# Layer 1 attention: the sums of the softmax over keys, taken by VectorE and transfers in place of a TensorE matmul

## The chip, the cores and the metric

The kernel runs on one core of a Trainium2 chip. The core has five engines with queues of their own: TensorE (PE in the profile; its weight loads are PEld), VectorE (DVE), ScalarE (ACT), GpSimd (POOL) and SyncE (SP, which here only issues transfers). Each queue is worked off in its order; an instruction that waits holds up those behind it. The metric is the time of one execution in microseconds of the device, the median of several runs.

## The reference, cut to what matters

Two gated layers work on x of shape (4, 1024, 512). Each adds to x the product of an attention branch and a feed-forward branch. The change touches the attention of layer 1 alone:

```python
q, k, v = (proj(wq), proj(wk), proj(wv))          # 16 heads of 32
q, k = apply_rope(q, k, sin, cos)
att = jnp.einsum('bhqd,bhkd->bhqk', q, k) * (1.0 / math.sqrt(HD))
att = jax.nn.softmax(att, axis=-1)
y = jnp.einsum('bhqk,bhkd->bhqd', att, v)
return y.transpose(0, 2, 1, 3).reshape(b, t, c) @ wo.T
```

The softmax divides by the sum over keys of exp(score - maximum). The kernel multiplies the exponentials with v first and divides afterwards, so it needs that sum for every head and query, as an inverse that stands in the layout of y.

## The kernel before, in words

**Units and steps.** The attention of layer 1 is cut into 32 units, (batch b, group g of 4 heads, half qh of the 1024 queries), in the order of the list `units` (L1085). Two units of the same heads are called a pair here: an even one (qh 0) and an odd one (qh 1). A unit has 8 steps, `TB`; one loop over s (L1110) runs through the 256 steps and 13 more, and the order of TensorE's instructions is the order in which this loop writes them. The order on the other engines and on the transfer queues is set by a planner, which lets a ready instruction of later in the program go first, except where `keep_in_program_order` pins one.

**A step on TensorE.** In step s come: the scores sq of unit s // 8 (`top`, L998), four heads in two tiles, from which VectorE takes the maxima over keys (L1011); y for the step e - 1 = s - 13 (`weigh`, L1052); one piece of a projection chain; the transposed scores sk of step e = s - 12 (`expo`, L1030), from which a second matmul with the maxima mT (L1043) subtracts and of which ScalarE takes the exponentials pT (L1048); three more pieces of the chain. `LAG` is 12. Where no chain is at hand, a step has none of these pieces.

**Chains.** `must` holds the projections of the next heads (wk and wq in two halves each, then v in two: six chains a pair), `spare` the output projections `wo_out` (L964) of a finished batch and half. A chain fills two steps. `left` (L1131) allows two output chains a pair; those that `soon` names for a step become available there. A wk or wq chain ends with a copy on ScalarE, eight small transfers on SP that swap rope's halves (L916), a product on VectorE (L919) and two operations on GpSimd (L920, L921).

**Buffers.** PSUM holds eight banks: `ring`, three tiles of two banks, taken in turn by sq and sk; `acc1`, one bank, for all chains; and one for y. The exponentials pT have three buffers in SBUF, the partial sums `part` two.

**The sums over keys.** For each unit GpSimd adds the eight pT tiles (128 keys x 4 heads x 512 queries) in seven additions (L1077, L1079), so that `part` holds, for each of 128 key rows, one partial sum. In step 6 of the unit after next (`zu`, L1192) TensorE finishes: `total` (L944) multiplies `part` by a matrix of ones, head by head, which leaves the sum over the 128 rows in z, already repeated on the 32 partitions that y has for this head. z stands in `acc1` (for the last of these units in `ring`). `divide` (L952) copies it to SBUF on ScalarE, inverts it on VectorE in four instructions of 128 columns, and GpSimd multiplies y's copy `yr` by it:

```python
zs = p2.tile([P, 512], F32, tag="zs", name=f"zs_{b}_{g}_{qh}", bufs=1)
nc.scalar.copy(zs, z)
...
    nc.vector.reciprocal(zs[:, cols], zs[:, cols])
nc.gpsimd.tensor_tensor(yT, yr, zs, ALU.mult)
```

This is so for units 0 to 29. The last two (`u >= nu - 2`) are summed on TensorE within their own steps. The maxima mT go a way that the change uses too: VectorE turns square blocks of 32 (L1016), four transfers write them to DRAM (`turned_d`, L1023), four read them back in the layout that is wanted (L1026).

Of the kernel before, what the change touches and what calls it, by code (L numbers as in the profile page):

```python
# [12 lines left out]
F32 = mybir.dt.float32  # L13
# [3 lines left out]
ALU = mybir.AluOpType  # L17
AX = mybir.AxisListType

P = 128  # L20
B, N, D = 4, 1024, 512
NT = B * N
H, HD = 16, 32
# [12 lines left out]
def kernel(ctx, tc, ins, out):  # L36
    nc = tc.nc
# [3 lines left out]
    dram = ctx.enter_context(tc.tile_pool(name="dram", bufs=1, space=bass.MemoryType.DRAM))  # L41
# [47 lines left out]
    def shared_tile(tag, name):  # L89
        return w0.tile([P, KD, D], F32, tag=tag, name=name)  # L90
# [155 lines left out]
    with ExitStack() as es:  # L246
# [4 lines left out]
        p2 = es.enter_context(tc.tile_pool(name="a0", bufs=2, reuse_waits="tile"))  # L251
# [318 lines left out]
    with ExitStack() as es:  # L570
# [3 lines left out]
        p2 = es.enter_context(tc.tile_pool(name="f0", bufs=2, reuse_waits="tile"))  # L574
# [126 lines left out]
        for g in range(NH0 * NBLK + 2 + 2 * TPB):  # L701
            blk, c = divmod(g, NH0)
            if g == NH0 * NBLK:

                for n in ("wk", "wq", "wv"):
# [3 lines left out]
                            out=W[n], in_=ins[n + "T"].rearrange("(k p) n -> p k n", p=P)  # L709
# [8 lines left out]
            for i in range(TPB):  # L718
                q = g - 2 - 2 * i
# [95 lines left out]
    with ExitStack() as es:  # L815
        wp = es.enter_context(tc.tile_pool(name="a1c", bufs=1, reuse_waits="tile"))
        p2 = es.enter_context(tc.tile_pool(name="a1", bufs=2, reuse_waits="tile"))

        def ring(name):
            return pp.tile([P, 2, 512], F32, tag="ring", name=name, bufs=3)  # L820

        def acc1(name):
            return pp.tile([P, 512], F32, tag="acc1", name=name)

        TB = N // P
# [4 lines left out]
        def load1(b):  # L830
            xnTs[b] = xpair(f"xnT1_{b}")
            for h in range(2):
                load = nc.sync.dma_start(
                    out=xnTs[b][h],
                    in_=xnT_d[b].rearrange("k p n -> p k n")[:, :, h * BLK : (h + 1) * BLK],
                )
                if b:
                    tc.keep_in_program_order(load)
# [7 lines left out]
        turned_d = [  # L846
            dram.tile([8, 512], F32, tag=f"turned{i}", name=f"turned_d{i}") for i in range(2)
        ]

        partner = []  # L850
        for i in range(2):
# [92 lines left out]
        def total(z, part, kb, n):  # L944

            for h in range(4):
                nc.tensor.matmul(  # L947
                    z[h * HD : (h + 1) * HD, :], lhsT=ones[:, :HD], rhs=part[:, h, :],
                    start=(kb == 0), stop=(kb == n - 1),
                )  # L950

        def divide(u, yr, z):  # L952

            b, g, qh = u
            zs = p2.tile([P, 512], F32, tag="zs", name=f"zs_{b}_{g}_{qh}", bufs=1)
            nc.scalar.copy(zs, z)
            yT = p2.tile([P, 512], F32, tag=f"yT{qh}", name=f"yT_{b}_{g}_{qh}", bufs=5 + qh)
            for c in range(TPB):
                cols = slice(c * P, (c + 1) * P)
                nc.vector.reciprocal(zs[:, cols], zs[:, cols])  # L960
            nc.gpsimd.tensor_tensor(yT, yr, zs, ALU.mult)
            yTs[b][g, qh] = yT
# [29 lines left out]
        def advance(parts):  # L992
            nonlocal chain
            for _ in range(parts):
                if chain is not None:
                    next(chain)
# [88 lines left out]
        units = [(b, g, qh) for b in range(B) for g in range(4) for qh in range(2)]  # L1085
        nu, LAG = len(units), TB + 4
        yTs = {b: {} for b in range(B)}
# [18 lines left out]
            tc.tile_pool(name="psuma", bufs=1, space=PSUM, reuse_waits="tile")  # L1106
        )
        must, spare = deque(), deque()
        mx, mTs, pTs, ys, parts, lates, soon = {}, {}, {}, {}, {}, {}, {}
        for s in range(TB * nu + LAG + 1):  # L1110

            e = s - LAG
            if s % (2 * TB) == 0 and s < TB * nu:

                assert not must
                n = s // (2 * TB) + 1
                if n < 4 * B:  # L1120
                    b, g = divmod(n, 4)

                    two = (nc.sync, nc.gpsimd) if s == 0 else (nc.sync, nc.sync)
                    must.extend(
                        heads_in(
                            b, g, acc1, {(w, h): two for w in ("wk", "wq") for h in range(2)}
                        )
                    )
                    if g == 3 and b + 1 < B:
                        load1(b + 1)  # L1130
                left = 2  # L1131
            if s in soon and s < TB * nu:
                spare.extend(wo_out(*soon.pop(s), acc1))
            if s % 2 == 0:

                chain = None
                if spare and left and s < TB * nu:
                    chain = spare.popleft()
                    left -= 1
                elif must:  # L1140
                    chain = must.popleft()
            if s == 2 * TB:
                W["wo"] = shared_tile("wo", "wo")
                tc.keep_in_program_order(
                    nc.sync.dma_start(
                        out=W["wo"], in_=ins["woT"].rearrange("(k p) n -> p k n", p=P)
                    )
                )
            if s % 4 == 0 and s // 4 < TPB:
                lates[s + 2] = s // 4, late(s // 4)  # L1150
            if s < TB * nu:
                u, j = divmod(s, TB)
                if j == 0:
                    mx[u] = p2.tile([P, TPB, 4, 2], F32, tag="mx", name=f"mx_{u}")
                for pair in range(2):
                    top(u, j, pair, mx[u])
                if j == TB - 1:
                    m2 = twice[u % 2][:, :, :8].rearrange("p q (h c) -> p q h c", c=2)

                    w = p2.tile([P, TPB, 4, 2], F32, tag="m1", name=f"m1_{u}")  # L1160
                    nc.vector.tensor_reduce(
                        w[:, :, :, 0], mx.pop(u), AX.X, ALU.max, negate=True
                    )
                    for out, sign in ((w[:, :, :, 1], -1.0), (m2[:, :, :, 0], 1.0)):
                        nc.scalar.activation(
                            out.bitcast(F32R), w[:, :, :, 0], AF.Copy, scale=sign
                        )
                    nc.vector.tensor_reduce(m2[:, :, :, 1], w, AX.X, ALU.add)
            late_exp = s >= TB * nu
            if late_exp:  # L1170
                exps(e)
            if 1 <= e <= TB * nu:
                u, kb = divmod(e - 1, TB)
                if kb == 0:
                    ys[u] = pp.tile([P, 512], F32, tag="y", name=f"y_{u}")
                weigh(u, kb, pTs[e - 1], ys[u])
                if u >= nu - 2:

                    if kb == 0:
                        z_last = acc1(f"z_{u}")  # L1180
                    if u < nu - 1 or kb < TB // 2:
                        total(z_last, pTs[e - 1], kb, TB)
                pTs.pop(e - 2, None)
                if kb == TB - 1:
                    yr = p2.tile([P, 512], F32, tag="yr", name=f"yr_{u}", bufs=1)
                    nc.scalar.copy(yr, ys[u])
                    ys[u] = yr
                    if u == nu - 2:
                        divide(units[u], ys.pop(u), z_last)
                        soon[s] = units[u][0], units[u][2], yTs[B - 1]  # L1190
            held = 0
            zu = (s - 6) // TB - 2  # L1192
            if s % TB == 0 and 0 < s <= TB * nu:
                turn_max(s // TB - 1)
            if s % TB == 6 and 0 <= zu < nu - 2:
                z = ring(f"z_{zu}")[:, 0, :] if zu == nu - 3 else acc1(f"z_{zu}")
                total(z, parts.pop(zu), 0, 1)
                divide(units[zu], ys.pop(zu), z)
                b, g, qh = units[zu]
                if g == 3:  # L1200
                    soon[s + 4] = b, qh, yTs[b]
            elif s in lates:
                late_turn(*lates.pop(s))
            else:
                held = 1
                advance(1)
            if not late_exp:
                exps(e)
            advance(4 - held)
            if TB * nu - 12 <= s < TB * nu:  # L1210

                nxt = weight(raw1, w0, True)
                if loaded:
                    loaded()
                loaded = nxt
                if s == TB * nu - 1:
                    loaded()

        soon = [*soon.values()]
# [307 lines left out]
```

## Time and profile before

| | us |
|---|---|
| median of 3 runs | 3089.14 (3086.78 to 3090.99) |
| the profiled execution | 3092.08 |
| its span, first to last instruction | 3090.2 |

| stretch of the span, us | PE | PEld | DVE | ACT | POOL |
|---|---|---|---|---|---|
| 600 to 1100 (end of layer 0) | 491.68 | 392.27 | 366.88 | 271.45 | 213.73 |
| 1300 to 1600 (attention, layer 1) | 296.69 | 115.07 | 166.93 | 127.87 | 265.14 |
| 1600 to 2000 | 400.00 | 159.46 | 220.57 | 171.10 | 342.99 |
| 2000 to 2500 | 497.84 | 198.38 | 277.11 | 218.16 | 436.26 |
| 2500 to 3090 (its end, feed-forward) | 574.63 | 434.80 | 329.63 | 201.75 | 60.30 |

The granted TensorE clock is 0.996 of full speed over the span. Columns are microseconds in which the engine was busy in that stretch. Matmuls are pipelined, so their spans overlap and a busy PE says nothing of how much it gets done. In lines of the timeline the columns are start, duration (both us), engine, line, operation, written and read tiles, shapes, count; in brackets stands the idle time ahead of the instruction and what ended it. In lines of groups, behind the bar: busy us, mean ns of one, idle us ahead of them and what ended most of it.

### The profile page before, as it was taken

How to read it: one execution, taken by the hardware profiler on the slowest of the kernel's cores; microseconds unless marked ns; L12 is line 12 of the kernel's file. 1: busy time of each engine (PE TensorE's matmuls, PEld its weight loads, DVE VectorE, ACT ScalarE, POOL GpSimd, SP SyncE). 2: the span in 40 equal slices, each digit the busy share in tenths (PEclk: the TensorE clock that was granted, in tenths of full speed). 3: DMA queues.
4: the chain of work that ended last, by engine and by line, in shares of the span. 5: the costliest groups of instructions: out<-in, count | busy, mean ns of one | idle time of the engine just before them, and what ended most of it. 6: DMA issues, size and time to landing. Idle time of an engine off the chain costs nothing.

```text
span 3090.2 us, 61139 instructions
## 1 busy us (share of the span) xinstructions
PE 3038.3 (98%) x25985; PEld 1730.5 (56%) x25985; DVE 1788.3 (58%) x2569; ACT 1173.7 (38%) x1708; POOL 1557.9 (50%) x742
## 2 busy tenths in 40 slices
PE   9999999999999998999999999999999999999998
PEld 5555555578788873333334444333434436888886
DVE  4444555467777776555555555555555544566655
ACT  3111111145556542444444444444444454333332
POOL 1221212234443444888888988888988940001001
PEclk9999999999999999999999999999999999999999
DMA  4222232323223231100001000100000014222111
GB/s 137 86 86 86 86 86 72 127 96 100 95 92 110 96 129 52 36 9 9 9 18 42 16 10 15 43 16 14 10 18 15 13 46 152 82 69 75 58 52 56
DMA packets 113787, 186.81 MB, mean 60 GB/s; under 512 B 19809, under 2 KB 33633, under 8 KB 113377
## 3 DMA queue, kind: packets, MB, share of 16 engines
q1 hardware_dynamic: 106096, 161.30, 17.3%
q0 software_dynamic: 7280, 21.39, 1.9%
q8 instruction: 205, 3.36, 0.5%
q14 instruction: 78, 0.63, 0.1%
q10 hardware_dynamic: 128, 0.13, 0.0%
HBM read 115.11 MB, written 59.26 MB: 56 GB/s over the span
## 4 chain that ended last, share of the span: by engine, by line
PE 57%; DVE 1%; ACT 1%; POOL 1%; issue 0%; SPq 0%; DMA 0%; ACTq 0%; POOLq 0%; DVEq 0%
PE sk L1037 9%; PE sq L1007 8%; PE y L1056 8%; PE gate L1260 5%; PE up L1260 5%; PE dn L1282 5%; PE wo L862 4%; PE v1ps L862 3%; PE wk L862 3%; PE wq L862 3%; PE sk L1043 2%; PE z L947 1%; ACT pT L1048 1%; DVE zs L960 1%; POOL part L1079 0%; DVE mx L1011 0%
## 5 line engine op out<-in xcount | busy, mean ns | idle before, releaser
L1011 DVE TENSOR_REDUCE mx<-sq 128x2 f32<-128x1024 f32 x512 | 604.2, 1218 | 434.8 <-PE sq L1007 434.0
L1079 POOL TENSOR_TENSOR part<-part,pT 128x2048 f32<-128x2048 f32 x180 | 817.8, 4543 | 17.3 <-ACT pT L1048 8.9
L1048 ACT ACTIVATE pT<-sk 128x1024 f32<-128x1024 f32 x512 | 495.6, 1020 | 557.3 <-PE sk L1043 520.1
L1007 PE MATMUL sq<-wkT,wqT 32*128 32x512 f32 x2048 | 321.0, 639 | 10.0 <-ACT pT L1048 7.0
L1037 PE MATMUL sk<-wqT,wkT 32*128 32x512 f32 x2048 | 322.8, 641 | 0.8 <-DVE mx L1011 0.5
L1056 PE MATMUL y<-pT,v 128*32 128x512 f32 x2048 | 275.5, 608 | 0.1
L1304 POOL TENSOR_TENSOR th<-th,x 128x512 f32<-128x512 f32 x31 | 40.1, 1293 | 458.0 <-DVE th L1303 379.0
L646 PE MATMUL pj<-wpj,hp 128*128 128x512 f32 x1024 | 262.0, 396 | 4.0 <-DVE hp L606 4.0
L593 PE MATMUL fc<-xp,wfc 128*128 128x512 f32 x1024 | 259.0, 395 | 3.6 <-ACT h L598 2.8
L614 POOL TENSOR_TENSOR sums<-sums,h 128x512 f32<-128x512 f32 x112 | 163.1, 1456 | 195.0 <-ACT h L598 189.7
L1043 PE MATMUL sk<-mT,onesr 2*128 2x512 f32 x1024 | 235.7, 788 | 0.0
L382 PE MATMUL qk<-xnT,wqkv 128*128 128x512 f32 x512 | 228.7, 600 | 0.7 <-ACT xnT L156 0.7
L646 PEld LDWEIGHTS pj<-wpj,hp 128*128 128x128 f32 x1024 | 191.2, 188 | 51.9 <-DVE hp L606 10.5
L593 PEld LDWEIGHTS fc<-xp,wfc 128*128 128x128 f32 x1024 | 189.4, 188 | 47.2 <-ACT h L598 6.0
L606 DVE TENSOR_TENSOR hp<-h,hp 128x512 fp32r<-128x512 f32 x128 | 128.2, 1001 | 85.2 <-ACT hp L603 85.2
L1260 PE MATMUL gate<-xp,wf 128*128 128x512 f32 x704 | 174.2, 390 | 0.0
L1260 PE MATMUL up<-xp,wf 128*128 128x512 f32 x704 | 173.9, 389 | 0.0
L1037 PEld LDWEIGHTS sk<-wqT,wkT 32*128 32x128 f32 x2048 | 96.2, 184 | 138.3 <-issue 117.2
L1282 PE MATMUL dn<-wf,hp 128*128 128x512 f32 x704 | 173.6, 390 | 0.0
L1077 POOL TENSOR_TENSOR part<-pT,pT 128x2048 f32<-128x2048 f32 x30 | 136.4, 4548 | 72.1 <-ACT pT L1048 72.0
L1007 PEld LDWEIGHTS sq<-wkT,wqT 32*128 32x128 f32 x2048 | 89.9, 184 | 122.7 <-issue 85.5
L382 PEld LDWEIGHTS qk<-xnT,wqkv 128*128 128x128 f32 x512 | 95.0, 191 | 111.8 <-issue 104.5
(230 smaller groups left out, 4359.3 us busy)
## 6 DMA issues: line engine op xcount, KB each, us to landing
s<-s SPq DMA_DIRECT2D x96, 256.0 KB
xp<-xp_d SPq DMA_DIRECT2D x16, 1024.0 KB
x<-x SPq DMA_DIRECT2D x36, 256.0 KB
x<-in_x SPq DMA_DIRECT2D x32, 256.0 KB
raw_fc<-in_w_fcT SPq DMA_DIRECT2D x32, 256.0 KB
xp_d<-hi POOLq DMA_DIRECT2D x32, 256.0 KB, 2.7
xp_d<-xnT POOLq DMA_DIRECT2D x32, 256.0 KB, 2.9
x0r<-in_x SPq DMA_DIRECT2D x32, 256.0 KB
```

The lines of the kernel that those rows point to most:

```text
L382: nc.tensor.matmul(a, lhsT=wqkv[k][:, c0 : c0 + P], rhs=xnTs[blk][:, k, :], start=(k == 0), stop=(k == KD - 1),)
L593: nc.tensor.matmul(a, lhsT=wfc[k][:, c * P : (c + 1) * P], rhs=xp[n][:, k, :].bitcast(F32R), start=(k == 0 and n == 0), stop=(k == KD - 1 ...
L646: nc.tensor.matmul(ds[i], lhsT=hparts[blk, c][n][:, i * P : (i + 1) * P], rhs=wpj[c], start=(c == 0 and n == 0), stop=(c == NH0 - 1 and n ...
L862: nc.tensor.matmul(out[r0 : r0 + HD, :], lhsT=lhsT[:, r0 : r0 + HD], rhs=rhs, start=start, stop=stop,)
L1007: nc.tensor.matmul(sq[:, hh, :], lhsT=qT[r, q0 : q0 + P], rhs=kT[r, n * 512 : (n + 1) * 512], start=True, stop=True,)
L1011: nc.vector.tensor_reduce(mx[:, qt, 2 * pair : 2 * pair + 2, n], sq, AX.X, ALU.max)
L1037: nc.tensor.matmul(sks[h // 2][:, h % 2, :], lhsT=kT[r, kb * P : (kb + 1) * P], rhs=qT[r, qh * 512 : (qh + 1) * 512], start=True, stop=False,)
L1048: nc.scalar.activation(pT[:, 2 * pair : 2 * pair + 2, :], sks[pair], AF.Exp, scale=QKS)
L1056: nc.tensor.matmul(y[r, :], lhsT=v[:, kb, r], rhs=pT[:, h, :], start=(kb == 0), stop=(kb == TB - 1),)
L1079: add.tensor_tensor(parts[u], parts[u], pT, ALU.add)
L1260: nc.tensor.matmul(a, lhsT=ws[n, c][:, k, :], rhs=xp[m][:, k, :], start=(k == 0 and m == 0), stop=(k == KD - 1 and m == 1),)
L1282: nc.tensor.matmul(ds[i], lhsT=hparts[blk, c][n][:, i * P : (i + 1) * P], rhs=w, start=(c == 0 and n == 0), stop=(c == NH1 - 1 and n == 1),)
```

## The change

For units 0 to 29 the matmul z, its copy and the four inverses are dropped. In their place, spread over steps from step 6 of the unit after next on (the same step in which z stood):

- `sums_of`, eight times a unit (two in step 6, then 1, 1, 2, 1, 1 in the steps after it): VectorE turns 256 of the 2048 columns of `part` in square blocks of 32, so that queries lie on partitions and the 32 key rows of one group of partitions lie in a row, and sums those rows to 8 columns of `groups`.
- `gather`, six steps after the first: VectorE turns `groups` back, a transfer writes it to DRAM (32 KB), and a second brings the four groups of key rows beside each other on 32 partitions.
- `invert`, two steps later: VectorE sums the four groups and inverts 64 columns; a transfer writes them to DRAM, and four transfers spread each head's 512 inverses on its 32 partitions (`partition_broadcast`).
- `times`, two steps later again: GpSimd's multiplication, as before.

So a unit's yT is there ten steps later than it was written before, and `soon` names the output chains for eight steps later. In the last pair `left` is 8. `yr` gets two buffers for one; `divide` stays for the last two units, with its zs in the buffers of mT.

```diff
+        groups_d = [dram.tile([P, 64], F32, tag=f"groups{i}", name=f"groups_d{i}") for i in range(2)]
+        inverse_d = [
+            dram.tile([2, HD, HD], F32, tag=f"inverse{i}", name=f"inverse_d{i}") for i in range(2)
+        ]
...
+        def sums_of(u, part, c):
+
+            if c == 0:
+                groups[u] = p2.tile([P, 64], F32, tag="groups", name=f"groups_{u}", bufs=1)
+            t = p2.tile([P, 256], F32, tag="keys", name=f"keys_{u}_{c}", bufs=1)
+            nc.vector.transpose(t, part.rearrange("p h q -> p (h q)")[:, c * 256 : (c + 1) * 256])
+            nc.vector.tensor_reduce(
+                groups[u][:, 8 * c : 8 * c + 8], t.rearrange("p (c a) -> p c a", a=HD), AX.X, ALU.add
+            )
+
+        def gather(u):
+            back = p2.tile([P, 64], F32, tag="back", name=f"back_{u}", bufs=1)
+            nc.vector.transpose(back, groups.pop(u))
+            at = groups_d[u % 2]
+            nc.sync.dma_start(out=at, in_=back)
+            sides[u] = p2.tile([P, 256], F32, tag="keys", name=f"sides_{u}", bufs=1)
+            nc.sync.dma_start(
+                out=sides[u][:HD, :].rearrange("c (i x) -> c i x", i=4),
+                in_=at.rearrange("(i c) x -> c i x", i=4),
+            )
+
+        def invert(u):
+            b, g, qh = units[u]
+            inv = p2.tile([P, 64], F32, tag="inv", name=f"inv_{u}", bufs=1)
+            nc.vector.tensor_reduce(
+                inv[:HD, :], sides.pop(u)[:HD, :].rearrange("c (i x) -> c x i", i=4), AX.X, ALU.add
+            )
+            nc.vector.reciprocal(inv[:HD, :], inv[:HD, :])
+            at = inverse_d[u % 2]
+            nc.sync.dma_start(
+                out=at.rearrange("a c b -> c a b"),
+                in_=inv[:HD, :].rearrange("c (a b) -> c a b", a=2),
+            )
+            zss[u] = p2.tile([P, 512], F32, tag="zs", name=f"zs_{b}_{g}_{qh}", bufs=1)
+            for h in range(4):
+                row = at[h // 2, 16 * (h % 2) : 16 * (h % 2) + 16, :]
+                nc.sync.dma_start(
+                    out=zss[u][h * HD : (h + 1) * HD, :],
+                    in_=row.rearrange("c b -> (c b)").partition_broadcast(HD),
+                )
+
+        def times(u, yr):
...
+            nc.gpsimd.tensor_tensor(yT, yr, zss.pop(u), ALU.mult)
+            yTs[b][g, qh] = yT
...
-            zs = p2.tile([P, 512], F32, tag="zs", name=f"zs_{b}_{g}_{qh}", bufs=1)
+            zs = p2.tile([P, 512], F32, tag="mT", name=f"zs_{b}_{g}_{qh}")
...
-                left = 2
+
+                left = 2 if n < 4 * B else TB
...
+            zu, at = divmod(s - 6, TB)
+            zu -= 2
+            for u, i in ((zu - 1, at + TB), (zu, at)):
+                if 0 <= u < nu - 2:
+                    if i < 6:
+                        for c in ((0, 1), (2,), (3,), (4, 5), (6,), (7,))[i]:
+                            sums_of(u, parts[u], c)
...
+                    elif i == 6:
+                        gather(u)
+                    elif i == 8:
+                        invert(u)
+                    elif i == 10:
+                        times(u, ys.pop(u))
+                        b, g, qh = units[u]
+                        if g == 3:
+                            soon[s + 2] = b, qh, yTs[b]
...
-                    yr = p2.tile([P, 512], F32, tag="yr", name=f"yr_{u}", bufs=1)
+                    yr = p2.tile([P, 512], F32, tag="yr", name=f"yr_{u}")
...
-            zu = (s - 6) // TB - 2
...
-            if s % TB == 6 and 0 <= zu < nu - 2:
-                z = ring(f"z_{zu}")[:, 0, :] if zu == nu - 3 else acc1(f"z_{zu}")
-                total(z, parts.pop(zu), 0, 1)
-                divide(units[zu], ys.pop(zu), z)
-                b, g, qh = units[zu]
-                if g == 3:
-                    soon[s + 4] = b, qh, yTs[b]
-            elif s in lates:
+            if s in lates:
```

More of the change, by code (lines that the diff above doesn't have):

```diff
@@ L952, in divide @@
+        def times(u, yr):
+            b, g, qh = units[u]
+            yT = p2.tile([P, 512], F32, tag=f"yT{qh}", name=f"yT_{b}_{g}_{qh}", bufs=5 + qh)
+            nc.gpsimd.tensor_tensor(yT, yr, zss.pop(u), ALU.mult)
+            yTs[b][g, qh] = yT
         def divide(u, yr, z):
             b, g, qh = u
-            zs = p2.tile([P, 512], F32, tag="zs", name=f"zs_{b}_{g}_{qh}", bufs=1)
+            zs = p2.tile([P, 512], F32, tag="mT", name=f"zs_{b}_{g}_{qh}")
             nc.scalar.copy(zs, z)
@@ L1108 @@
         must, spare = deque(), deque()
+        groups, sides, zss = {}, {}, {}
         mx, mTs, pTs, ys, parts, lates, soon = {}, {}, {}, {}, {}, {}, {}
@@ L1168 @@
                     nc.vector.tensor_reduce(m2[:, :, :, 1], w, AX.X, ALU.add)
+            zu, at = divmod(s - 6, TB)
[5 more added lines that the diff above has]
+                            sums_of(u, parts[u], c)
+                        if i == 5:
+                            parts.pop(u)
+                    elif i == 6:
[4 more added lines that the diff above has]
+                        times(u, ys.pop(u))
+                        b, g, qh = units[u]
+                        if g == 3:
+                            soon[s + 2] = b, qh, yTs[b]
             late_exp = s >= TB * nu
```

## The prediction

> **What bounds the kernel now.** I read the page first, then the timeline of layer 1's attention (1162 to 2570 us of the span) engine by engine, then its groups of instructions with shapes kept apart, then the waits.
>
> ```profile
> PE 3038.3 (98%) x25985; PEld 1730.5 (56%) x25985; DVE 1788.3 (58%) x2569; ACT 1173.7 (38%) x1708; POOL 1557.9 (50%) x742
> PE sk L1037 9%; PE sq L1007 8%; PE y L1056 8%; PE gate L1260 5%; PE up L1260 5%; PE dn L1282 5%; PE wo L862 4%; PE v1ps L862 3%; PE wk L862 3%; PE wq L862 3%; PE sk L1043 2%; PE z L947 1%; ACT pT L1048 1%; DVE zs L960 1%; POOL part L1079 0%; DVE mx L1011 0%
> ```
>
> PE sets the end nearly everywhere, and the two things that the change takes away, the matmul z (L947) and the inverses (L960), each have about 1% of the chain. What a piece of PE work is worth is read from the steps: every step begins with the matmuls sq, so the distance between two such starts is its length.
>
> ```profile
> 1821.50 1.14 PE L1007 MATMUL sq<-wkT,wqT 32*128 32x512 f32 x8
> 1826.76 1.14 PE L1007 MATMUL sq<-wkT,wqT 32*128 32x512 f32 x8
> 1828.71 1.04 PE L947 MATMUL z<-part,ones 128*32 128x512 f32 x8
> 1832.87 1.14 PE L1007 MATMUL sq<-wkT,wqT 32*128 32x512 f32 x8
> ...
> 1782.21 1.14 PE L1007 MATMUL sq<-wkT,wqT 32*128 32x512 f32 x8
> 1788.42 1.14 PE L1007 MATMUL sq<-wkT,wqT 32*128 32x512 f32 x8
> ...
> 1804.69 1.14 PE L1007 MATMUL sq<-wkT,wqT 32*128 32x512 f32 x8
> 1810.47 1.14 PE L1007 MATMUL sq<-wkT,wqT 32*128 32x512 f32 x8
> ...
> 2494.70 1.02 PE L1007 MATMUL sq<-wkT,wqT 32*128 32x512 f32 x4
> ```
>
> Odd unit 15: 5.26 us without z, 6.11 with it, and again 5.25 after it (next start 1838.12). Even unit 14: its z step takes 6.21, but there a wk or wq chain has just ended, and such a step takes 5.78 without z too. The last line begins a step with no projection chain, and the next start is at 2499.29: 4.59 us, held not by PE's work but by the three-buffer ring (sq waits for the exponentials). With z two such steps take 5.45 and 5.28 (starts at 1303.49, 1308.94, 1314.22).
>
> **What is removed: 24.1 us.** I read the starts of all 256 steps. (a) Even units 2 to 28: 14 x (6.21 - 5.78) = 6.0. (b) Odd units 11 to 29 outside the idle steps: 10 x (6.12 - 5.24) = 8.8, and unit 19's z step took 7.07, so 1.0 more. (c) Units 3, 5, 7, where z falls into chainless steps: 3 x (5.45 + 5.28 - 2 x 4.59) = 4.6. (d) Output chains start later (steps 82, 146, 210 for 74, 138, 202), so two of them leave pair 4 (units 8, 9) and come in pair 15. Unit 9 was 43.4; with four chainless steps like unit 3's, less z, it is 38.9, but the first step of unit 10 becomes 6.7 for 5.2 as after unit 3: 3.0 gained. (e) Unit 30 gets two more chains: eight steps of 5.24 and a transition step of 3.59 for 44.5 before: 1.0 lost. (f) Unit 31's z step, 6.31 against 4.59: 1.7. The ACT copy of z (0.585) and 128 - 8 inverses go too; their worth is inside these differences.
>
> **What VectorE gains and loses.** The rows:
>
> ```profile
> L1011 DVE TENSOR_REDUCE mx<-sq 128x2 f32<-128x1024 f32 x512 | 604.2, 1218 | 434.8 <-PE sq L1007 434.0
> ...
> L960 DVE RECIPROCAL zs<-zs 128x128 f32<-128x128 f32 x128 | 108.3, 908 | 35.7 <-ACT zs L956 35.7
> ...
> L1016 DVE STREAM_TRANSPOSE mt<-m 128x128 f32<-128x128 f32 x32 | 10.0, 312 | 3.0
> ...
> 1786.26 3.38 DVE L960 RECIPROCAL zs<-zs 128x128 f32<-128x128 f32 x4
> 1789.60 2.35 DVE L1011 TENSOR_REDUCE mx<-sq 128x2 f32<-128x1024 f32 x2
> ```
>
> The reduce of the maxima takes 1218 ns for 1024 elements and L1161, a reduce of 32, takes 186: a slope of (1218 - 186)/(1024 - 32) = 1.04 ns an element, so 256 elements take 0.42. No transpose of 256 columns is in the trace; it lies between 0.31 (L1016, 128) and 0.69 (L919, 512 columns), and with the reduces' slope at 0.45. Eight pairs: 8 x 0.87 = 6.9 a unit. The back transpose of 64 columns is 0.25, the second reduce 0.42, the inverse of 64 columns (between 0.18 for 4, L121, and 0.91 for 128) 0.5. Dependent instructions stand 0.09 apart (L1168 to L1016 at 1792.46): some 1.6. Together 9.7 for 3.4 of inverses, 6.3 more per unit. VectorE idles 2.88 a step ahead of mx, 23 a unit, so the sum is covered. The cover that matters is the single step: in step 6 of a unit two pairs (1.9) and the inverting (1.1) come to 3.0. The block of 3.38 in the fence above is a bound: mx followed it 0.1 late, and the next step was 5.24. That z step was 0.4 to 0.9 longer than the new ones, so I take 0.1 a unit for 26 units (0 to 0.6), and for the four units in chainless steps, where an mx 3.39 late did show (L960 at 1308.57 is in the chain of waits), 0.8 each: 5.8 us in all.
>
> [...]
>
> **The transfers.** Seven DMAs per unit are put on SP's queue, and two of its waits are new: the read of groups_d waits for its write, the four spreads wait for inverse_d. The nearest row is the transfer of the maxima, and for what a queue loses behind a transfer, a rope product on POOL:
>
> ```profile
> 1793.07 2.77 SPq L1023 DMA_DIRECT2D turned_d<-mt  x4
> 1797.08 0.85 SPq L1026 DMA_DIRECT2D mT<-turned_d  x3
> 1804.83 1.27 POOL L920 TENSOR_TENSOR rr<-rr,cs 128x512 f32<-128x512 f32 x1 [1.61 <-DMA rr<-raw_wk]
> ```
>
> A write's issue takes 0.66, and 1.24 after the last one the read goes out: 1.9. A rope transfer lands 1.45 after its last issue of 0.62 (1788.80 to 1790.25): 2.1. So back transpose, write and read are 0.25 + 1.9 + 2.1 = 4.3 us, the second trip with its four reads 1.9 + 4 x (0.25 to 0.66) + 1.5 = 4.4 to 6.0. The code puts two steps, 10.5 us, between gather and invert, and between invert and times. Eight rope issues in front (5.4) still fit: 9.7. SP is busy 32 us of a pair's 87 (32 rope issues, two turnings); 4.2 to 7.1 a unit more is room enough, and moves one rope half by about 0.7. In the last units SP also waits on weight buffers (up to 6.2 us each, L777): 2 us.
>
> [...]
>
> But order in a queue is not program order: the turning transpose L1016, written behind a step's mx, ran ahead of them. If invert is put before an mx and its transfer lands later, mx and then PE stand. The lower bound is 0 (the trip above fits). The upper one is POOL's L920, which waited for transfers 32 of 54 times, 74.6 us in the waits view, 2.3 each. I take 0, nearest to the trip that fits, and keep 30 x 2.3 = 70 for the range. The sums wait for part as z did (12 waits of 0.5), from a queue where mx stands behind them: inside the same bounds.
>
> **POOL** keeps its multiply (1.27). A pair costs it 14 x 4.54 + 10 x 1.27 = 76 us, with a pair now 85.9: it stays covered while its waits stay under 9; today they are about 10 of 87, half of them for want of work.
>
> **Sum.** 24.1 - 5.8 - 2 = 16. Profiled execution 3092.1 (span 3090.2) - 16 = 3076. It stood 2.9 above the median 3089.1, which makes 3073.
>
> **The rivals.** *More is gained* (0.06): the idle steps lose the stalls behind the inverses too, 4 x (6.7 - 5.2) = 6, and nothing is given back: 3089 - 24 - 6 = 3059 or below, to 3054. For it: 6.7 comes four times right after 3.39 us of inverses. Against: the same step waits for the exponentials.
> *Nothing* (0.09): times waits in POOL's queue as L920 does. In odd units the adds already run up to 8.8 us behind their exponentials, and three pT buffers allow about 11; 2.3 more can stall each of 14 pairs by 1.2: 16, 3089. Against: two steps of distance, and the lag drains in every pair.
> *Slower* (0.37): VectorE's queue stands at the second reduce, or at the first transpose of part, with the next mx behind it and then the ring. Sign turns at 16/30 = 0.53 us of PE stall per unit, 0.2% slower at 0.74. Half of L920's wait and a little, 1.3 us, gives 39: 3112; all of it 3143. For it: VectorE serves PE within 0.1 us and now waits for transfers and for POOL. Against: 2.88 us idle in every step, half the price is swallowed there.
>
> **How the numbers follow.** Forecast (0.48): 3073, own range 3057 to 3083, which leaves its costs between 0 and 18. From the slower case the range takes in all but its last third, from the larger gain most: 3056 to 3128. A measurement of this kernel tells 0.2% (6 us) from no change: 3083 to 3095 is the same. Faster 0.54, same 0.09, slower 0.37.
>
> **What would show it.** z leaves the chain; sq starts in step 6 come 5.24 (odd) and 5.78 (even) apart; L960 is 8 instructions; VectorE's new pieces are near 0.43. I am wrong if mx gets idle time released by a DMA or by POOL's part, and sq or sk by mx, of over 0.5 us a unit; or if transposes of 256 take over 0.6.

## The result, and the profile after

| | before | after |
|---|---|---|
| median, us (6 runs each) | 3091.34 (3086.78 to 3098.83) | 3492.68 (3489.61 to 3502.39) |
| span of the profiled run, us | 3090.2 | 3493.2 |
| granted TensorE clock over the span | 0.996 | 0.936 |
| last y matmul of layer 1 ends at, us | 2569.3 | 2972.4 |

The changed kernel takes 1.1303 times as long (95% interval 1.1282 to 1.1324). The whole loss, 403 us, lies in the attention of layer 1; what follows it keeps its length.

The page of the changed kernel: engine shares, granted clock, and the chain of waits by engine and by line.

```profile
PE 3187.8 (91%) x25745; PEld 1771.1 (51%) x25745; DVE 1929.9 (55%) x3019; ACT 1159.8 (33%) x1678; POOL 1557.7 (45%) x742
...
PEclk9999999999999997889898988899888989999999
...
PE 38%; POOL 10%; DVE 8%; SPq 3%; issue 3%; DMA 2%; ACT 1%; POOLq 0%; ACTq 0%; DVEq 0%
...
L965 DVE STREAM_TRANSPOSE keys<-part 128x256 f32<-128x256 f32 x240 | 106.5, 444 | 230.8 <-POOL part L1134 224.6
```

PE no longer sets the end alone: it is busy for 91% of the span, 98% before, and GpSimd and VectorE are on the chain with 10% and 8%, where each had 1% before. The last line is the new transpose: each one is short (444 ns), but VectorE stood idle for 224.6 us in front of them, for GpSimd's additions to part. The waits of VectorE, then of PE and of its weight loads, from 1270 to 2990 us (total us, times, longest):

```profile
DVE keys L965 <- POOL part L1134: 218.5, 29, 15.6
...
DVE inv L984 <- DMA sides<-groups_d: 37.8, 30, 3.4
...
PE sq L1062 <- DVE mx L1066: 145.5, 25, 9.7
PE sk L1092 <- DVE mx L1066: 104.9, 30, 11.1
...
PEld sq L1062 <- DVE mx L1066: 156.7, 27, 10.0
PEld sk L1092 <- DVE mx L1066: 147.4, 77, 11.9
```

One wait a unit for part, 7.5 us each in the mean, and behind it PE waits for the maxima. For nearly the same work, PE in the two kernels, before and after (the length of the stretch, then PE's busy time with its instructions, those of PEld, DVE, ACT and POOL, and the granted clock, the DMA share and GB/s):

```profile
1300.00:2550.00 1250.00, 1242.29 (x14966) 487.70 (x14968) 684.38 (x711) 548.20 (x699) 1062.05 (x331) 1.00 0.07 19
```
```profile
1300.00:2950.00 1650.00, 1396.56 (x14924) 534.91 (x14924) 826.44 (x1150) 538.46 (x674) 1075.60 (x335) 0.88 0.08 20
```

Of these 400 us PE stands idle for 246 (253.4 for 7.7). In the other 154 it is busy longer, at a clock of 0.88; the last section shows what slowed it.

Where in the unit the loss falls is read from the distances between the starts of sq, step by step, as in the prediction. Means over units 8 to 29, us:

| step of the unit | 0 | 1 | 2 | 3 | 4 | 5 | 6 | 7 | sum |
|---|---|---|---|---|---|---|---|---|---|
| before, even units | 5.37 | 5.24 | 5.38 | 5.24 | 5.38 | 5.24 | 6.20 | 5.24 | 43.3 |
| after, even units | 5.48 | 5.23 | 5.43 | 5.24 | 8.81 | 12.68 | 5.67 | 5.23 | 53.8 |
| before, odd units | 5.81 | 5.24 | 5.63 | 5.23 | 5.64 | 5.25 | 6.20 | 5.25 | 44.3 |
| after, odd units | 5.81 | 5.24 | 5.72 | 5.24 | 14.75 | 12.41 | 5.89 | 5.20 | 60.3 |

Steps 4 and 5 of a pair lose 3.4 + 7.4 + 9.1 + 7.2 = 27.1 us; 15 pairs make 407. Step 6, where the sums are written, is shorter without z: 5.67 and 5.89 us, where 5.78 and 5.24 were foreseen. VectorE's timeline in step 4 and 5 of unit 16 shows what stands there (start, duration, and in brackets the idle time ahead and its end):

```profile
2058.01 1.22 DVE L1066 TENSOR_REDUCE mx<-sq 128x2 f32<-128x1024 f32 x1 [2.88 <-PE sq L1062]
2062.23 0.45 DVE L965 STREAM_TRANSPOSE keys<-part 128x256 f32<-128x256 f32 x1 [3.00 <-POOL part L1134]
2062.71 0.42 DVE L966 TENSOR_REDUCE groups<-keys 128x8 f32<-128x256 f32 x1
2063.05 1.22 DVE L1066 TENSOR_REDUCE mx<-sq 128x2 f32<-128x1024 f32 x1
2064.18 0.43 DVE L965 STREAM_TRANSPOSE keys<-part 128x256 f32<-128x256 f32 x1
...
2070.25 0.42 DVE L966 TENSOR_REDUCE groups<-keys 128x8 f32<-128x256 f32 x1
2070.70 0.24 DVE L972 STREAM_TRANSPOSE back<-groups 128x64 f32<-128x64 f32 x1
2070.87 2.32 DVE L1066 TENSOR_REDUCE mx<-sq 128x2 f32<-128x1024 f32 x2
```

The first transpose, written in step 6, runs between the two maxima of step 4, when GpSimd hasn't finished part: 3.0 us of idle here, 9.6 in the unit before, and the second maximum of the step stands behind it. The other seven pairs and the back transpose, written over the steps 6 to 12, run in one block from 2064.18 to 2070.9, ahead of step 5's maxima. The planner has moved the sequence two steps forward and closed it up.

### The profile page after: what moved, and what is told of

The parts are those of the page before. It is cut to its first block, busy times and chain, and to the rows that moved or that the text cites. A ratio compares the mean times of both kernels' runs of the same rounds, so it can differ in the third digit from the quotient of the medians.

```text
span 3493.2 us, 61412 instructions
## 1 busy us (share of the span) xinstructions
PE 3187.8 (91%) x25745; PEld 1771.1 (51%) x25745; DVE 1929.9 (55%) x3019; ACT 1159.8 (33%) x1678; POOL 1557.7 (45%) x742
## 4 chain that ended last, share of the span: by engine, by line
PE 38%; POOL 10%; DVE 8%; SPq 3%; issue 3%; DMA 2%; ACT 1%; POOLq 0%; ACTq 0%; DVEq 0%
POOL part L1134 8%; PE sk L1092 6%; PE sq L1062 5%; PE gate L1328 5%; PE up L1328 5%; PE dn L1350 4%; PE y L1111 4%; DVE keys L965 3%; PE wo L866 3%; SPq L920 3%; DVE groups L966 3%; DVE mx L1066 3%; PE v1ps L866 2%; PE wk L866 2%; PE sk L1098 1%
## 5 line engine op out<-in xcount | busy, mean ns | idle before, releaser
L1062 PE MATMUL sq<-wkT,wqT 32*128 32x512 f32 x2048 | 365.3, 715 | 158.6 <-DVE mx L1066 150.9
L1092 PE MATMUL sk<-wqT,wkT 32*128 32x512 f32 x2048 | 393.6, 682 | 105.7 <-DVE mx L1066 105.4
L1111 PE MATMUL y<-pT,v 128*32 128x512 f32 x2048 | 299.8, 658 | 0.1
L1098 PE MATMUL sk<-mT,onesr 2*128 2x512 f32 x1024 | 277.7, 826 | 0.0
L1092 PEld LDWEIGHTS sk<-wqT,wkT 32*128 32x128 f32 x2048 | 113.7, 195 | 271.7 <-DVE mx L1066 149.5
L1062 PEld LDWEIGHTS sq<-wkT,wqT 32*128 32x128 f32 x2048 | 100.2, 204 | 284.1 <-DVE mx L1066 162.9
L965 DVE STREAM_TRANSPOSE keys<-part 128x256 f32<-128x256 f32 x240 | 106.5, 444 | 230.8 <-POOL part L1134 224.6
```

The source lines that it names most:

```text
L1062: nc.tensor.matmul(sq[:, hh, :], lhsT=qT[r, q0 : q0 + P], rhs=kT[r, n * 512 : (n + 1) * 512], start=True, stop=True,)
L1092: nc.tensor.matmul(sks[h // 2][:, h % 2, :], lhsT=kT[r, kb * P : (kb + 1) * P], rhs=qT[r, qh * 512 : (qh + 1) * 512], start=True, stop=False,)
L1098: nc.tensor.matmul(sks[h // 2][:, h % 2, :], lhsT=onesr[r, :], rhs=mTs[u][r, :].bitcast(F32R), start=False, stop=True,)
L1111: nc.tensor.matmul(y[r, :], lhsT=v[:, kb, r], rhs=pT[:, h, :], start=(kb == 0), stop=(kb == TB - 1),)
```

## Experiments

Two theories. **Order**: the operations are affordable where they are written; what costs 400 us is the order that the planner gave VectorE's queue, by a wait (step 4) and by a block (step 5). **Work**: VectorE's pieces and the seven transfers a unit are too much for this stage wherever they stand. All times below stand beside runs of the kernel before on the same chip: medians of 3093.61 us for pin_all, pin_block, no_z and no_z_late, 3095.13 for pin_early, pin_four, pin_no_trip and pin_dve, 3092.42 for pin_light, pin_act and pin_light_act. pin_block, pin_early and pin_four have two runs each; their losses are far outside the spread of these.

**pin_all.** The new operations of VectorE, and GpSimd's multiplication, are held where they are written; nothing else differs.

```diff
-            nc.vector.transpose(t, part.rearrange("p h q -> p (h q)")[:, c * 256 : (c + 1) * 256])
...
+            tc.keep_in_program_order(
+                nc.vector.transpose(t, part.rearrange("p h q -> p (h q)")[:, c * 256 : (c + 1) * 256])
+            )
...
+            tc.keep_in_program_order(nc.gpsimd.tensor_tensor(yT, yr, zss.pop(u), ALU.mult))
```

> The changed kernel with every new VectorE instruction and the multiplication of times held in the order in which the loop writes them; nothing else differs. Theory A (order: the planner let the sums go ahead from step 6 to step 4, where VectorE waits for POOL's part, and put all eight pairs in one block in front of a step's mx): some 3073 us, 0.4 to 0.8% under the kernel before, steps 4 and 5 of a unit back at 5.24 to 5.78, no idle time of VectorE that POOL's part ends, granted clock back above 0.98. Theory B (the work itself: VectorE's 8 us a unit, seven more transfers on SP, POOL behind the inverses): it stays above 3300.

Measured: 3090.6 us, ratio 0.9992 (0.9976 to 1.0008). The same instructions in another order take 402 us less: the loss is the order. VectorE's wait for part is gone, steps 4 and 5 are back at 5.2 to 5.8. But the gain, 3073 by the expectation, doesn't appear either. What is left of a loss shows in the first step of the even units, 6.31 for 5.37, and in ScalarE's waits for GpSimd (1300 to 2550 us), first of the kernel before, then of this one:

```profile
ACT pT L1048 <- POOL part L1079: 8.5, 3, 3.5
```
```profile
ACT pT L1109 <- POOL part L1140: 44.5, 11, 4.3
...
ACT pT L1109 <- POOL part L1138: 11.2, 10, 1.3
```

The exponentials wait for a pT buffer that GpSimd hasn't read yet: GpSimd's lag, covered before, has become a bound in these steps. pin_dve below relieves GpSimd and tests this.

**pin_block.** As pin_all, but all eight pairs in step 6.

```diff
-                        for c in ((0, 1), (2,), (3,), (4, 5), (6,), (7,))[i]:
+                        for c in (range(8), (), (), (), (), ())[i]:
```

> As pin_all, but all eight pairs of sums are written and held in step 6 of the unit, where part is ready. Theory A: no wait for POOL, but six or more pairs (5.6 us) and the inverting (1.1 us) stand between the mx of step 6 and those of step 7, with 2.9 us of idle time to take them in, so PE stands 4 to 5 us a unit: 3190 to 3230. If the wait for POOL was the whole loss, the block costs nothing and it comes out like pin_all. Theory B: above 3300.

Measured: 3308.33 us, ratio 1.069 (1.0658 to 1.0722), +215 us, with no wait for part at all. VectorE, unit with step 7 at 2332:

```profile
2328.06 2.36 DVE L1072 TENSOR_REDUCE mx<-sq 128x2 f32<-128x1024 f32 x2 [2.90 <-PE sq L1068]
2330.33 0.59 DVE L989 TENSOR_REDUCE inv<-sides 32x64 f32<-32x256 f32 x1
...
2338.71 2.35 DVE L1072 TENSOR_REDUCE mx<-sq 128x2 f32<-128x1024 f32 x2
```

The block takes 8.4 us. The maxima should have started 5.26 after the last ones, at 2333.3; they are 5.4 late, and the step takes 13.0 for 5.24: 7.75 more. The block alone is worth half of the loss. The expectation, 3190 to 3230, was missed: it counted the block's length against the idle time, and the step loses more than that (last section). The time lies in the range that it gave to the theory of work, above 3300, but pin_all has the same work and 3090.6.

**pin_early.** As pin_all, but the sequence is written two steps earlier: the wait without the block.

```diff
-            zu, at = divmod(s - 6, TB)
+            zu, at = divmod(s - 4, TB)
```

> As pin_all, held in program order and paced as there, but the whole sequence from sums_of to times is written two steps earlier, so the first pair stands in step 4, where the planner had put it. No block, only the wait for part. Theory A (waiting in VectorE's queue costs PE what it lasts, less the idle time): in odd units part is ready some 12.6 us after the start of step 4 and VectorE is there after 4.6, so 8 us and more are lost in each of 14, and under 1 in each even one: 3210 to 3260. If the block alone made the loss: within 10 us of pin_all (3091).

Measured: 3253.49 us, ratio 1.0515 (1.0491 to 1.0539), +158 us. VectorE's waits from 1270 to 2800 us have:

```profile
DVE keys L966 <- POOL part L1140: 126.6, 29, 8.1
```

The odd units carry it: their step 5 takes 14.9, against 5.25; the even ones lose 1.2 there. Wait and block, 158 and 215, together make 373 of the 401. Both are real causes; that the sum comes so near is partly luck, since neither run copies its part exactly: the wait is 4.4 us a unit here and 7.5 in the changed kernel, and pin_block's block holds eight pairs and the inverting, not seven pairs and the back transpose.

**pin_four.** As pin_all, four pairs in step 6 and four in step 0.

```diff
+                        for c in ((0, 1, 2, 3), (), (4, 5, 6, 7), (), (), ())[i]:
```

> As pin_all, but four pairs in step 6 and four in step 0 in place of 2, 1, 1, 2, 1, 1. Theory A with the idle time of 2.9 us as the measure: step 6 then holds 4 x 0.92 + 1.1 = 4.8 us, 1.9 over, step 0 holds 3.7, 0.8 over; 2.7 us a unit, 80 us: 3160 to 3180. If a PE that stands briefly loses no clock, no more than that. If the block's price was one of length alone (7.2 us a unit for eight pairs, so 3.6 for each four): 3300.

Measured: 3151.74 us, ratio 1.0186 (1.0158 to 1.0214), +57 us. In step 6 the block (inverting and four pairs) ends 1.7 us after the maxima are due, and step 7 takes 6.9, 1.7 more; the clock over the span stays at 0.99. Here a small lateness costs its own length (see the last section for larger ones). The expectation, 3160 to 3180, was a little high.

**no_z** and **no_z_late.** The kernel before without z, its copy and the inverses: units 0 to 29 are multiplied by ones, so they stay undivided. no_z_late has the later output chains and `left` of the change as well.

```diff
-                z = ring(f"z_{zu}")[:, 0, :] if zu == nu - 3 else acc1(f"z_{zu}")
-                total(z, parts.pop(zu), 0, 1)
-                divide(units[zu], ys.pop(zu), z)
+                parts.pop(zu)
...
+                nc.gpsimd.tensor_tensor(yT, ys.pop(zu), level, ALU.mult)
```

> The kernel before, without the matmul z, its copy and the four inverses for units 0 to 29; POOL multiplies y by a tile of ones, so these units are left undivided. It prices what the change takes away, with the output chains where they were: by the terms a, b, c and f of the prediction's sum 21 us, so 3066 to 3072. If chains, bank and VectorE hid z (the rival that nothing is gained): within 6 us of the kernel before.

> As no_z, with the output chains eight steps later and left at 8 in the last pair, as in the changed kernel; also left undivided. The prediction's terms d and e give 2 us more, so 3064 to 3070, within 0.2% of no_z. It is the floor that the changed kernel could reach with all its new work hidden.

Measured: 3077.08 us, ratio 0.9948 (0.9931 to 0.9966), and 3080.36 us, 0.9954 (0.9937 to 0.997). So all that is removed is worth 14 to 16 us, not 24, and both expectations were missed. The even units show where (no_z, units 8 to 29): their z step falls from 6.20 to 5.87, but their first step rises from 5.37 to 5.65, and their sum stays (43.28, 43.25); the odd ones gain 0.87. GpSimd's work in a pair is unchanged, and ScalarE's waits for it rise from 8.5 to 12.0 us (1300 to 2550 us); that PE gives back in the even units what it gained by way of pT's buffers fits this, but no run isolates it. The later chains give nothing that can be told.

**pin_no_trip.** As pin_all, without the seven transfers; VectorE's operations stay, units 0 to 29 stay undivided.

```diff
-            nc.sync.dma_start(out=at, in_=back)
...
+            zss[u] = level
```

> As pin_all with the seven transfers of a unit left out: VectorE does all its work, the second reduce reads a tile of ones, POOL multiplies by that tile, so units 0 to 29 are left undivided. It parts what is left between pin_all (3091) and no_z_late (3080). If the transfers are the rest (SP's queue with two more waits, rope late on POOL, exponentials behind POOL's adds): 3074 to 3082, as no_z_late. If VectorE's work is: 3088 to 3093.

Measured: 3085.03 us, ratio 0.9973 (0.9962 to 0.9984). Set beside the others by ratios, since they ran on different chips, that lies in the middle between no_z_late (0.9954) and pin_all (0.9992), and between the two outcomes that were expected: VectorE's work costs some 0.0019, 6 us, and so do the transfers. The intervals of neighbours touch, so each 6 is an estimate. For the transfers the trace of pin_all names one place: GpSimd's rope product waits until a trip is over (1300 to 2550 us), which fits rope transfers that stand behind the trips in SP's queue; that this is the whole 6 us is only argued:

```profile
POOL rr L924 <- DMA inverse_d<-inv: 23.7, 9, 2.9
```

**pin_dve.** As pin_all, with the multiplication on VectorE, to relieve GpSimd.

```diff
+            tc.keep_in_program_order(nc.vector.tensor_tensor(yT, yr, zss.pop(u), ALU.mult))
```

> As pin_all, with the multiplication of times on VectorE in place of POOL, held in program order. POOL is at its limit by the theory of the rest: 2.5 us less of it a pair and no wait for the inverses there, so its adds run less late and the exponentials wait less than 56 us: 3076 to 3084, faster than both kernels. If VectorE has no room for 0.7 to 1.0 us more, or waits for the inverses: 3090 or more.

Measured: 3098.56 us, ratio 1.0011 (1.0001 to 1.002): expectation missed. The relief itself worked: the first step of the even units falls from 6.31 to 5.78, and ScalarE's waits for GpSimd from 58.9 to 15.6 us. But their second step rises from 5.23 to 6.93, because of the multiplication. The rope product L923 of the same size takes 0.69 on VectorE, every time; this multiplication takes from 0.68 to 4.96. The longest one on VectorE, and GpSimd at that time:

```profile
2375.71 4.96 DVE L1010 TENSOR_TENSOR yT<-yr,zs 128x512 f32<-128x512 f32 x1
```
```profile
2370.93 14.12 POOL L1140 TENSOR_TENSOR part<-part,pT 128x2048 f32<-128x2048 f32 x3
```

In the trace's single records the second of these three additions runs from 0.14 before the multiplication's start to 4.41 after it, and the multiplication ends 0.55 later. The others are alike: 27 of the 30 start while an addition runs, and each of them ends 0.55 to 0.66 after that addition does. So the multiplication waits inside the instruction for GpSimd's addition, and no wait shows in any list. The rope product doesn't: 42 of its 64 start while such an addition runs, and none takes over 0.69. One of its two inputs lies in PSUM; both of the multiplication's lie in SBUF. Whether that makes the difference was not shown.

**pin_light.** As pin_all, with pairs per step 1, 0, 2, 1, 2, 2, so that the step of the inverting carries one pair.

```diff
+                        for c in ((0,), (), (1, 2), (3,), (4, 5), (6, 7))[i]:
```

> As pin_all, but the step in which the inverting stands (step 6) gets one pair of the next unit, not two, and the step after it none: pairs per step 1, 0, 2, 1, 2, 2 for 2, 1, 1, 2, 1, 1. Theory: what pin_all still loses against no_z_late (12 us, of which 6 are VectorE's part) comes from the 3.0 us block in front of the maxima that end a unit, which makes mT and the rope transfers behind it late, and with them POOL and the exponentials' buffers. Then the first step of the even units falls from 6.31 to about 5.8 and the time by 4 to 7 us against pin_all: ratio 0.997 to 0.998. Rival: these steps are long because POOL has too much work in a pair, wherever VectorE's pieces stand: ratio as pin_all, 0.999, and the first steps stay at 6.3.

Measured: 3089.12 us, ratio 0.9987 (0.9975 to 1.0); the first step of the even units is 6.23, as the rival said. The block of 3.0 in step 6 wasn't what holds these steps; ScalarE still waits 45.7 us for GpSimd's additions (L1140).

**pin_act** and **pin_light_act.** The reads of both trips on ScalarE's queue, one and two steps after their writes; the multiplication two steps later.

```diff
-            nc.sync.dma_start(
+            nc.scalar.dma_start(
                 out=sides[u][:HD, :].rearrange("c (i x) -> c i x", i=4),
...
-                nc.sync.dma_start(
+                nc.scalar.dma_start(
                     out=zss[u][h * HD : (h + 1) * HD, :],
```

> As pin_all, but the read of groups_d is issued one step after its write, the four spreads two steps after the write of the inverses, both on ScalarE's queue, and the multiplication two steps later (12 for 10). SP's queue keeps the two writes alone. Theory: the transfers cost pin_all 5.5 us (3090.6 against pin_no_trip's 3085) by SP's waits of 30 x 3.0 and 30 x 3.0 us ahead of rope transfers, so this gives 3085 to 3088, ratio 0.997 to 0.998, and POOL's wait for inverse_d (23.7 us) goes. Rival: five more issues a unit on ScalarE hold the exponentials, and PE waits for them: above pin_all, ratio over 1.0.

> Both of the edits above. If the two losses are separate, their gains add: 3079 to 3083, ratio 0.995 to 0.996, as no_z_late. If POOL's load is the limit, the ratio stays at 0.998 to 0.999.

Measured: 3203.4 us, ratio 1.0361 (1.0338 to 1.0384), and 3201.49 us, 1.0359 (1.0345 to 1.0374). The rival, at a higher price. ScalarE's waits in pin_act from 1300 to 2650 us:

```profile
ACT pT L1116 <- DMA groups_d<-back: 36.9, 13, 4.3
ACT yr L1279 <- POOL yT L1017: 32.4, 10, 4.6
ACT m L1235 <- DMA zs<-inverse_d: 25.8, 5, 5.9
ACT m L1235 <- issue: 21.1, 4, 5.7
```

Now the exponentials and the turning of the maxima stand behind a transfer, and the copy yr behind the later multiplication; the runs make both changes and don't part them. The same mistake on another engine: a wait went into a queue that PE depends on. No version that was run is faster than the kernel before and computes the whole result; pin_light and pin_all equal it.

## Why the prediction was wrong, step by step

**The step that failed** is the one on the order of the queue: "The lower bound is 0 (the trip above fits)... I take 0, nearest to the trip that fits, and keep 30 x 2.3 = 70 for the range. The sums wait for part as z did (12 waits of 0.5), from a queue where mx stands behind them: inside the same bounds." The same paragraph begins by saying that order in a queue is not program order, and then prices the sums at their written place. In fact they ran two steps ahead of it, and the wait was 29 x 7.5 us, not 12 x 0.5. An upper bound from L920's waits (2.3) couldn't hold this. The first transpose went into step 4, right behind step 3, where the last addition to its part is written, so the row to take was that addition: 4.54 us long, and begun up to 8.8 us behind its exponentials, the lag that the prediction itself names under the second rival. After the change, part of unit 14 is finished 5.4 us after step 4 of unit 16 begins, that of unit 13 12.6 us after step 4 of unit 15. pin_all and pin_early show that this wait was the cost.

**The spread** failed in the same way. "The cover that matters is the single step" was right, and 2.88 of idle too; that step 6 would hold two pairs was taken from the loop. Seven pairs came in one step. pin_block prices a block of eight at 7.2 us a unit; pin_four, with four, loses in step 7 no more than its lateness.

**The slower rival** (0.37) had the mechanism word for word, the queue standing "at the first transpose of part, with the next mx behind it and then the ring". Its price was at most 2.3 us a unit against 13.4 measured (403/30): the wait was larger, the block wasn't in it, and PE's stands cost more than their length (7.75 us for one of 4.2 in pin_block).

**The wait that was feared**, invert for its transfer, came (37.8 us, 30 times, 1.26 each), and it hurt nothing: step 6 that follows takes 5.67 and 5.89, step 7 5.2.

**The working that stood** once the order is held. Pieces: transposes 444 ns (0.45 predicted), reduces 420 (0.42), back transpose 245 (0.25), second reduce 586 (0.42 predicted; it reads 32 partitions in strides, and whether that makes it longer was not shown), inverses 541 (0.5). VectorE's cost: 5.8 predicted, some 6 measured. Transfers: 2 predicted, for the last units; some 6 measured, and not there: in units 8 to 29 a pair takes 87.2 us in pin_all and 86.6 in pin_no_trip. Removed: 24.1 predicted, 14 to 16 measured; of its terms (a), the even units' 6.0, gave 3.2 in no_z's trace and nothing net from unit 8 on, and (d) nothing that can be told. In the written order, then, 16 was forecast and pin_all has 3.0: 13 too much. The measured terms, 14 - 6 - 6 = 2, must come near that, since each 6 is a difference of these same runs. The line "it stays covered while its waits stay under 9" about GpSimd missed that the lag isn't spread over the pair: it shows in the first step of the even units.

Which cost or due time made the planner place the sums so early wasn't tried.

## What to carry to other kernels

Where a planner orders an engine's queue, price a new instruction at the earliest place that its inputs allow, and at the wait that it would have there, or pin it; an engine with 2.9 us of slack a step is safe only for work whose place is fixed. When several small pieces stand ahead of an instruction that the bound engine waits for, price them as one block as well as spread. And before counting what the bound engine gains, ask which engine is next: here GpSimd, 76 of 86 us busy in a pair, took back part of it.

## What the runs showed of the hardware

**A stall of 4.2 us cost more than its length.** Of the changed kernel, the granted clock in stretches of 2 us (columns as above; the clock is the third number from the end):

```profile
2066.00:2068.00 2.00, 1.94 (x20) 0.43 (x8) 1.83 (x6) 0.00 (x0) 0.00 (x0) 1.00 0.00 0
2068.00:2070.00 2.00, 0.00 (x0) 0.00 (x0) 1.86 (x5) 0.00 (x0) 0.00 (x0) 1.00 0.00 0
2070.00:2072.00 2.00, 0.00 (x0) 0.00 (x0) 1.93 (x5) 0.00 (x0) 0.00 (x0) 0.60 0.07 16
2072.00:2074.00 2.00, 1.89 (x8) 0.84 (x8) 1.19 (x2) 0.00 (x0) 0.00 (x0) 0.50 0.08 17
2074.00:2076.00 2.00, 2.00 (x20) 0.77 (x20) 1.12 (x2) 1.69 (x2) 0.00 (x0) 0.50 0.00 0
2076.00:2078.00 2.00, 2.00 (x24) 0.53 (x16) 0.00 (x0) 0.83 (x2) 1.68 (x1) 0.69 0.07 17
2078.00:2080.00 2.00, 2.00 (x24) 0.66 (x22) 1.99 (x3) 0.00 (x0) 2.00 (x1) 1.00 0.47 118
```

PE stops near 2067.9 and starts again at 2072.1. By the shares of 0.60 and 0.69, the clock falls to half at 2070.4, 2.5 us into the stand, and comes back at 2077.2, 5.1 us after the restart; the 24 chain matmuls at 2074.54 take 2.79 us, those of the step before 1.50. In pin_block's step above PE stands for 4.2 us, and 6.4 of the 6.8 us at half rate fall behind the restart: half of 6.4 is lost, and 4.2 + 3.2 = 7.4 is nearly the 7.75. The step 7 of pin_four runs at the full clock in all but one of the units 10 to 29 and loses 1.7 for 1.7. A safe length can't be read from this: in the changed kernel a stand of 1.5 us (from 1733.1) was followed by 3.4 us at half rate (from 1735.9), and one of 2.2 us (from 2062.1) by none. Each of the 49 stretches at half rate in the changed kernel's attention lasts 3.41 us or a multiple of it: 7 last 3.41, 25 last 6.83 as the one here, the longest 23.89.

**VectorE waited inside an instruction** (pin_dve): the multiplication, 0.68 us at its shortest, took up to 4.96 while GpSimd added.
